# Moving part of a kernel's input loads to another DMA queue, with a different split over rows

## The chip, the cores and the metric

The kernel runs on one core of one Trainium2 chip. The metric is device time in microseconds (us), the median of several runs. A core has five engines that run their own instruction streams: TensorE (PE in the profile; its weight loads are PEld), VectorE (DVE), ScalarE (ACT), GpSimd (POOL) and SyncE (SP). Beside them sixteen DMA engines carry data between HBM and the on-chip memory. A DMA is issued by one of the instruction streams and then cut into packets, which the sixteen engines work off.

## The reference

For 1024 batch rows there are 32 fields of 128 numbers. For each of the 496 pairs of fields i < j the kernel multiplies field i by a 128x128 matrix that belongs to the pair, and multiplies the result elementwise by field j.

```python
# r_inputs: (1024, 32, 128) f32     L0_rec_W: (496, 128, 128) f32
v_i = inputs[:, I_IDX, :]
v_j = inputs[:, J_IDX, :]
transformed = jnp.einsum('bpd,ped->bpe', v_i, W)
return transformed * v_j            # (1024, 496, 128) f32
```

The output is 1024 x 496 x 128 x 4 bytes = 260.05 MB. The inputs are 16.8 MB (fields) and 32.5 MB (matrices). Almost all of the traffic is output.

## The kernel before

The host has transposed the data: a field is a tile of 128 partitions (rows) with 1024 numbers each, so one row of a field is 4 KB, and one field is 512 KB. Pairs are worked off in the order i = 30, 29, ... 0, so that field i is first needed when its row of pairs begins, and each field is loaded once, into a tile of its own.

```python
def _pairs():
    return [(i, j) for i in range(NF - 2, -1, -1) for j in range(i + 1, NF)]
...
xpool = ctx.enter_context(tc.tile_pool(name="x", bufs=1))
rpool = ctx.enter_context(tc.tile_pool(name="wr", bufs=5))
opool = ctx.enter_context(tc.tile_pool(name="o", bufs=4))
ppool = ctx.enter_context(tc.tile_pool(name="ps", bufs=8, space=bass.MemoryType.PSUM))
...
def load_x(f, n=1, pieces=1, eng=None):
    t = xpool.tile([P, n, BT], F32, tag=f"x{f}", name=f"x_{f}")
    s = BT // pieces
    for k in range(pieces):
        (eng or nc.sync).dma_start(out=t[:, :, k * s : (k + 1) * s], in_=xt[:, f : f + n, k * s : (k + 1) * s])
    ...
def load_w(c, splits=(0, WL)):        # WL = 4 matrices, 256 KB, 2 KB a row
    ...
        nc.sync.dma_start(out=w_raw[c][:, a:b, :], in_=wt[c, :, a:b, :])
```

The first eight fields (31 down to 24) and four groups of matrices are loaded ahead of the loop. The loop counts half pairs: u = 2q + h is half h (512 of 1024 columns) of pair q. A product in full precision takes three matmuls on split operands (the first 15 pairs use one native matmul). GpSimd does most of the splitting.

```python
def second(u):
    ...                                # third matmul into po[u]
    if k == 0 and h == 0:
        ots[g] = opool.tile([P, OG, BT], F32, tag="ot", name=f"ot_{g}")   # OG = 2 pairs, 1 MB, 8 KB a row
    nc.vector.tensor_tensor(ots[g][:, k, s], po.pop(u), x_sb[j][:, s], ALU.mult)
    ...
    elif k == OG - 1 and h == 1:
        nc.sync.dma_start(out=out[g], in_=ots[g])

for u in range(2 * NQ + LAG):          # NQ = 496
    q = u // 2
    if u % (2 * WL) == 0 and (q // WL + WLEAD) * WL < NQ:
        load_w(q // WL + WLEAD)
    if u < 2 * NQ:
        i, j = pairs[q]
        if u % 2 == 0 and j == i + 1 and 0 <= i - 2 - XLEAD:   # XLEAD = 5
            load_x(i - 2 - XLEAD)      # fields 23 down to 0
        first(u)
    if u >= LAG:
        second(u - LAG)
    ...                                # one split of matrices or of a field
```

So each group of two pairs takes four VectorE multiplications and ends in one 1 MB output DMA; four output tiles are in turn. The in-loop loads of fields 23 to 0 are issued at u = 0, 2, 6, 12, 20, 30, ... 506, 552 (of 992), seven rows of pairs ahead of their use.

Of the kernel before, what the change touches and what calls it, by code (L numbers as in the profile page):

```python
# [1 line left out]

# [4 lines left out]

F32 = mybir.dt.float32
F32R = mybir.dt.float32r
ALU = mybir.AluOpType  # L10

P = 128
NF = 32
NQ = NF * (NF - 1) // 2
BT = 1024
HB = 512
WC = 2
WL = 4
OG = 2
EPS = 2.0**-12  # L20
NATIVE = 5
SHARED = 10
XDLAG = 10
LAG = 3
WLEAD = 4
XLEAD = 5


def _pairs():

    return [(i, j) for i in range(NF - 2, -1, -1) for j in range(i + 1, NF)]


@with_exitstack
def kernel(
    ctx: ExitStack,
    tc: tile.TileContext,
    xt: bass.AP,
    wt: bass.AP,
    out: bass.AP,  # L40
):

    nc = tc.nc
    pairs = _pairs()
    nchunk = NQ // WC  # L60

    xpool = ctx.enter_context(tc.tile_pool(name="x", bufs=1))
    spool = ctx.enter_context(tc.tile_pool(name="xs", bufs=2))
    rpool = ctx.enter_context(tc.tile_pool(name="wr", bufs=5))
    wpool = ctx.enter_context(tc.tile_pool(name="ws", bufs=4))
    opool = ctx.enter_context(tc.tile_pool(name="o", bufs=4))
    ppool = ctx.enter_context(tc.tile_pool(name="ps", bufs=8, space=bass.MemoryType.PSUM))

    x_sb = {}
# [6 lines that stand above are left out]
            (eng or nc.sync).dma_start(out=t[:, :, k * s : (k + 1) * s], in_=xt[:, f : f + n, k * s : (k + 1) * s])  # L76
        for k in range(n):
            x_sb[f + k] = t[:, k, :]

    w_raw = {}  # L80

    def load_w(c, splits=(0, WL)):
        w_raw[c] = rpool.tile([P, WL, P], F32, tag="w", name=f"w_{c}")
        for a, b in zip(splits, splits[1:]):
            nc.sync.dma_start(out=w_raw[c][:, a:b, :], in_=wt[c, :, a:b, :])  # L85

    w_s = {}

    def split_w(c, u):

        k = c * WC % WL
        raw = w_raw[c * WC // WL][:, k : k + WC, :].rearrange("p q e -> p (q e)")
        h, l, d = [wpool.tile([P, WC * P], F32R, tag=t, name=f"{t}_{c}") for t in ("wh", "wl", "wd")]
        nc.scalar.mul(h, raw, 1.0 - 2.0**-13)  # L94
        nc.gpsimd.tensor_tensor(l, raw, h.bitcast(F32), ALU.subtract)  # L95
        nc.gpsimd.tensor_scalar(d, h.bitcast(F32), EPS, 1.0, ALU.mult, ALU.mult)  # L96
        nc.gpsimd.tensor_tensor(d, l.bitcast(F32), d.bitcast(F32), ALU.subtract)  # L97
        w_s[c] = (h, l, d)

    x_s = {}  # L100
    later = []

    def split_x(f, a, u):

        if a == 0:
            x_s[f] = [spool.tile([P, BT], F32R, tag=t, name=f"{t}_{f}") for t in ("xh", "xl", "xd")]
        s = slice(a, a + HB)
        h, l, d = [t[:, s] for t in x_s[f]]
        nc.scalar.mul(h, x_sb[f][:, s], 1.0 - 2.0**-13)  # L109
        nc.gpsimd.tensor_tensor(l, x_sb[f][:, s], h.bitcast(F32), ALU.subtract)  # L110
        nc.gpsimd.tensor_scalar(l, l.bitcast(F32), 1.0 / EPS, 1.0, ALU.mult, ALU.mult)  # L111
        if f > NF - 2 - NATIVE - SHARED:
            later.append((min(u + XDLAG, 2 * first_q[f] + LAG - 1), d, h.bitcast(F32), l.bitcast(F32)))
        else:
            nc.gpsimd.tensor_tensor(d, h.bitcast(F32), l.bitcast(F32), ALU.subtract)  # L115

    nq0 = NATIVE * (NATIVE + 1) // 2
    c0 = nq0 // WC
    first_q = {i: q for q, (i, j) in reversed(list(enumerate(pairs)))}

    todo = []
    for c in range(c0, nchunk):
        todo.append(((c - 3) * WC + 1, max(c * WC, nq0), lambda u, c=c: split_w(c, u)))
    for i in range(NF - 2 - NATIVE, -1, -1):
        for a in range(0, BT, HB):
            todo.append((first_q[i + 1] + 1 if i < NF - 3 - NATIVE else 2, first_q[i], lambda u, i=i, a=a: split_x(i, a, u)))
    todo.sort(key=lambda t: t[1])

    load_w(0, (0, 1, WL))
    load_x(NF - 2, pieces=2, eng=nc.scalar)
    load_x(NF - 1, pieces=2, eng=nc.scalar)
    load_x(NF - 3)
    load_x(NF - 4)
    load_w(1)
    for f in range(NF - 5, NF - 4 - XLEAD, -1):
        load_x(f)
    load_w(2)
    load_w(3)  # L140


    ctx.enter_context(tc.manual_schedule())
    po, ots = {}, {}


    def first(u):
        q, h = divmod(u, 2)
        i, c = pairs[q][0], q // WC
        r = slice(q % WC * P, (q % WC + 1) * P)  # L150
        s = slice(h * HB, (h + 1) * HB)
        po[u] = ppool.tile([P, HB], F32, tag="po", name=f"po_{u}")
        if q < nq0:
            nc.tensor.matmul(po[u], w_raw[q // WL][:, q % WL, :], x_sb[i][:, s], start=True, stop=True)  # L154
        else:
            for t in (0, 1):
                nc.tensor.matmul(po[u], w_s[c][t][:, r], x_s[i][t][:, s], start=t == 0, stop=t == 1)  # L157
            nc.scalar.mul(po[u], po[u], 1.0 + EPS)  # L158

    def second(u):  # L160
        q, h = divmod(u, 2)
        i, j = pairs[q]
        r = slice(q % WC * P, (q % WC + 1) * P)
        s = slice(h * HB, (h + 1) * HB)
        if q >= nq0:
            nc.tensor.matmul(  # L166
                po[u], w_s[q // WC][2][:, r], x_s[i][2][:, s], start=False, stop=True, skip_group_check=True
            )
        g, k = divmod(q, OG)
        if k == 0 and h == 0:  # L170
            ots[g] = opool.tile([P, OG, BT], F32, tag="ot", name=f"ot_{g}")
        nc.vector.tensor_tensor(ots[g][:, k, s], po.pop(u), x_sb[j][:, s], ALU.mult)  # L172
        if q >= NQ - 2:
            nc.sync.dma_start(out=out[g, :, k, s], in_=ots[g][:, k, s])
        elif k == OG - 1 and h == 1:
            nc.sync.dma_start(out=out[g], in_=ots[g])

    for u in range(2 * NQ + LAG):
# [3 lines that stand above are left out]
        if u < 2 * NQ:  # L182
            i, j = pairs[q]
            if u % 2 == 0 and j == i + 1 and 0 <= i - 2 - XLEAD:
                load_x(i - 2 - XLEAD)
            first(u)
        if u >= LAG:
            second(u - LAG)
        if u % 2 == 1:
            ready = [t for t in todo if t[0] <= q]  # L190
            if ready:
                ready[0][2](u)
                todo.remove(ready[0])
        while later and later[0][0] <= u:
            nc.vector.tensor_tensor(*later.pop(0)[1:], ALU.subtract)  # L195
    assert not todo and not later


# [25 lines left out]
```

## Time and profile before

The median of three runs is 768.14 us (766.21 to 768.76). The profiled execution has a span of 769.8 us.

| engine | busy us | share of the span |
|---|---|---|
| PE (matmul) | 722.7 | 94% |
| ACT | 638.7 | 83% |
| DVE | 632.0 | 82% |
| POOL | 593.2 | 77% |

The busy time of an engine is the union of its instructions' times. That of PE is modelled for pipelined matmuls and overstates how near PE is to its peak. The DMA engines are not in this table; the page reports them by slices and by queue. All in-loop loads and all stores are issued by SyncE, and so lie in one hardware queue (q1), which spreads every transfer over the sixteen DMA engines[...].

### The profile page before, as it was taken

The page shows a single profiled execution, that of the slowest core. Times are in us where ns is not written, and L with a number is a line of the kernel's source. Part 1 is how long each engine was busy: PE and PEld are TensorE (multiplying, and loading weights), DVE is VectorE, ACT ScalarE, POOL GpSimd, SP SyncE. Part 2 cuts the span into 40 slices and gives each one's busy share as a digit, 9 for nine tenths or more (in the row PEclk, how much of TensorE's full clock was granted, in tenths as well). Part 3 has the DMA queues.
Part 4 walks back from the last instruction along what each step waited for, and adds up shares of the span by engine and source line. Part 5 has one row for each costly group of instructions (what it writes and reads, how often), then busy time and mean ns, then how long its engine had stood idle before and what let it go on. Part 6 is the DMA issues. An engine that isn't in the chain of part 4 may idle for free.

```text
span 769.8 us, 11824 instructions
## 1 busy us (share of the span) xinstructions
PE 722.7 (94%) x2946; PEld 545.4 (71%) x2946; DVE 632.0 (82%) x1012; ACT 638.7 (83%) x1256; POOL 593.2 (77%) x863
## 2 busy tenths in 40 slices
PE   7988999999999999999999989999999999999994
PEld 3556766677777676777777767777777777777773
DVE  4869888888888788888888878888888888888885
ACT  2276988888888898888888889998988898998983
POOL 2677998887889878878878696978786969697660
PEclk9999999999999999999999999999999999999998
DMA  9999999999999999999999999999999999999997
GB/s 352 424 419 384 407 397 410 405 400 406 410 405 403 400 409 416 409 379 421 411 414 407 412 403 406 411 407 408 415 410 395 408 410 409 409 408 405 400 401 307
DMA packets 59108, 310.11 MB, mean 403 GB/s; under 512 B 6560, under 2 KB 6816, under 8 KB 27424
## 3 DMA queue, kind: packets, MB, share of 16 engines
q1 hardware_dynamic: 58464, 308.31, 99.4%
q10 hardware_dynamic: 576, 1.05, 0.4%
q8 instruction: 24, 0.39, 0.2%
q14 instruction: 44, 0.36, 0.1%
HBM read 49.28 MB, written 260.05 MB: 402 GB/s over the span
## 4 chain that ended last, share of the span: by engine, by line
DMA 61%; DVE 21%; PE 15%; issue 2%; DVEq 0%; SPq 0%; ACT 0%
DMA out_dram<-ot 60%; DVE ot L172 19%; PE po L157 9%; PE po L166 4%; DVE xd L195 2%; PE po L154 1%; DMA x<-in_xt_dram 1%; DVEq L172 0%; SPq L85 0%; DVEq L217 0%; ACT po L158 0%; DVEq L195 0%
## 5 line engine op out<-in xcount | busy, mean ns | idle before, releaser
L172 DVE TENSOR_TENSOR ot<-po,x 128x512 f32<-128x512 f32 x992 | 618.6, 684 | 129.5 <-DMA out_dram<-ot 70.2
L158 ACT ACTIVATE po<-po 128x512 f32<-128x512 f32 x962 | 551.2, 583 | 106.5 <-PE po L157 53.3
L157 PE MATMUL po<-xh,wh 128*128 128x512 f32 x962 | 388.7, 404 | 24.4 <-DVE ot L172 21.6
L166 PE MATMUL po<-xd,wd 128*128 128x512 f32 x962 | 376.9, 392 | 5.7 <-DVE xd L195 5.7
L157 PE MATMUL po<-xl,wl 128*128 128x512 f32 x962 | 377.6, 392 | 2.2 <-POOL wl L95 2.1
L157 PEld LDWEIGHTS po<-xh,wh 128*128 128x128 f32 x962 | 180.9, 188 | 110.2 <-DVE ot L172 72.5
L95 POOL TENSOR_TENSOR wl<-w,wh 128x256 fp32r<-128x256 f32 x241 | 179.2, 744 | 92.1 <-ACT wh L94 90.7
L166 PEld LDWEIGHTS po<-xd,wd 128*128 128x128 f32 x962 | 181.0, 188 | 46.3 <-ACT po L158 3.8
L157 PEld LDWEIGHTS po<-xl,wl 128*128 128x128 f32 x962 | 181.1, 188 | 36.8 <-POOL wl L95 4.5
L97 POOL TENSOR_TENSOR wd<-wl,wd 128x256 fp32r<-128x256 f32 x241 | 180.0, 747 | 20.1
L96 POOL TENSOR_SCALAR wd<-wh 128x256 fp32r<-128x256 f32 x241 | 99.1, 411 | 20.3
L94 ACT ACTIVATE wh<-w 128x256 fp32r<-128x256 f32 x241 | 99.2, 412 | 0.5 <-DMA w<-in_wt_dram 0.5
L110 POOL TENSOR_TENSOR xl<-x,xh 128x512 fp32r<-128x512 f32 x52 | 67.3, 1293 | 19.8 <-ACT xh L109 19.5
L115 POOL TENSOR_TENSOR xd<-xh,xl 128x512 fp32r<-128x512 f32 x32 | 41.4, 1292 | 2.7
L109 ACT ACTIVATE xh<-x 128x512 fp32r<-128x512 f32 x52 | 32.5, 628 | 10.5 <-DMA x<-in_xt_dram 10.3
L111 POOL TENSOR_SCALAR xl<-xl 128x512 fp32r<-128x512 f32 x52 | 32.8, 631 | 4.6
L154 PE MATMUL po<-x,w 128*128 128x512 f32 x60 | 29.0, 645 | 4.1 <-DMA x<-in_xt_dram 4.1
L154 PEld LDWEIGHTS po<-x,w 128*128 128x128 f32 x60 | 12.1, 206 | 20.2 <-issue 13.9
L195 DVE TENSOR_TENSOR xd<-xh,xl 128x512 fp32r<-128x512 f32 x20 | 16.6, 831 | 0.0
L109 ACT ACT_TABLE_LOAD x1 | 1.3, 1283 | 2.6 <-issue 2.6
L211 POOL MEMSET const-float32-0.0<- 128x1 f32 x1 | 0.1, 98 | 0.2 <-issue 0.2
L211 POOL MEMSET const-bfloat16-1.0<- 128x1 bf16 x1 | 0.1, 101 | 0.0
(2 smaller groups left out, 0.2 us busy)
## 6 DMA issues: line engine op xcount, KB each, us to landing
out_dram<-ot SPq DMA_DIRECT2D x247, 1024.0 KB, 8.9
w<-in_wt_dram SPq DMA_DIRECT2D x123, 256.0 KB, 9.1
x<-in_xt_dram SPq DMA_DIRECT2D x30, 512.0 KB, 9.5
x<-in_xt_dram ACTq DMA_DIRECT2D x4, 256.0 KB, 5.1
out_dram<-ot SPq DMA_DIRECT2D x4, 256.0 KB, 7.0
w<-in_wt_dram SPq DMA_DIRECT2D x1, 192.0 KB, 3.6
w<-in_wt_dram SPq DMA_DIRECT2D x1, 64.0 KB, 2.9
```

Of the source, the lines that this page charges most:

```text
L94: nc.scalar.mul(h, raw, 1.0 - 2.0**-13)
L95: nc.gpsimd.tensor_tensor(l, raw, h.bitcast(F32), ALU.subtract)
L96: nc.gpsimd.tensor_scalar(d, h.bitcast(F32), EPS, 1.0, ALU.mult, ALU.mult)
L97: nc.gpsimd.tensor_tensor(d, l.bitcast(F32), d.bitcast(F32), ALU.subtract)
L109: nc.scalar.mul(h, x_sb[f][:, s], 1.0 - 2.0**-13)
L110: nc.gpsimd.tensor_tensor(l, x_sb[f][:, s], h.bitcast(F32), ALU.subtract)
L115: nc.gpsimd.tensor_tensor(d, h.bitcast(F32), l.bitcast(F32), ALU.subtract)
L154: nc.tensor.matmul(po[u], w_raw[q // WL][:, q % WL, :], x_sb[i][:, s], start=True, stop=True)
L157: nc.tensor.matmul(po[u], w_s[c][t][:, r], x_s[i][t][:, s], start=t == 0, stop=t == 1)
L158: nc.scalar.mul(po[u], po[u], 1.0 + EPS)
L166: nc.tensor.matmul(po[u], w_s[q // WC][2][:, r], x_s[i][2][:, s], start=False, stop=True, skip_group_check=True)
L172: nc.vector.tensor_tensor(ots[g][:, k, s], po.pop(u), x_sb[j][:, s], ALU.mult)
```

## The change

The 24 fields that the loop loads are no longer loaded by one SyncE DMA of 128 rows. Rows 0 to 119 are loaded by a DMA that GpSimd issues ([...], in a queue of its own), and rows 120 to 127 by a small DMA of SyncE. The aim is to split these loads over the DMA engines in another way than the other transfers and to take them out of SyncE's queue. The bytes are the same, as are the tiles and the place in program order.

```diff
+XROWS = 120
...
+    def load_x_by_two(f):
+
+        t = xpool.tile([P, BT], F32, tag=f"x{f}", name=f"x_{f}")
+        nc.gpsimd.dma_start(out=t[:XROWS], in_=xt[:XROWS, f, :])
+        nc.sync.dma_start(out=t[XROWS:], in_=xt[XROWS:, f, :])
+        x_sb[f] = t
...
             if u % 2 == 0 and j == i + 1 and 0 <= i - 2 - XLEAD:
-                load_x(i - 2 - XLEAD)
+                load_x_by_two(i - 2 - XLEAD)
             first(u)
```

## The prediction

> **What bounds the kernel now.** I read the page's slices and queues first, then the chain, then the waits, and then stretches of the loop.
>
> ```profile
> DMA  9999999999999999999999999999999999999997
> GB/s 352 424 419 384 407 397 410 405 400 406 410 405 403 400 409 416 409 379 421 411 414 407 412 403 406 411 407 408 415 410 395 408 410 409 409 408 405 400 401 307
> q1 hardware_dynamic: 58464, 308.31, 99.4%
> ```
>
> The sixteen DMA engines have a packet in hand all the time, but they do not always move equally much: 424 and 419 GB/s in the second and third slice, some 408 later. Same busy share, 4% less moved, so packets got longer. That gap is what I want to explain. The chain of work by time shows how the DMA sets the pace:
>
> ```profile
> 516.95 2.50 DVE ot L172 x4
> 519.45 0.02 issue
> 519.47 8.95 DMA out_dram<-ot
> 528.41 0.03 issue
> 528.44 0.05 DVEq L172
> ...
> 744.18 0.23 PE po L166
> 744.41 0.71 PE po L157 x2
> ```
>
> Four multiplications fill an output tile (2.50 us), its store takes 8.95 us, and the chain goes on with the multiplication that needs the tile back. Four tiles are in turn, so one round of 16 multiplications takes about 11.5 us. The wait list says the same (first column: who waited for whom, total us, times, longest):
>
> ```profile
> DVE ot L172 <- DMA out_dram<-ot: 70.2, 83, 2.1
> DVE ot L172 <- PE po L166: 30.3, 34, 1.6
> ```
>
> Where no store holds it (744 us), the compute side needs 0.68 us a multiplication (0.23 for L166 and 0.45 for the mean pair of L157). The pace of the loop, from the multiplications in two stretches, one with field loads and one without:
>
> ```profile
> L172 DVE TENSOR_TENSOR ot<-po,x x263: 678/681/693, 199.5 to 399.4; 128x512 f32<-128x512 f32 x132
> L76 SPq DMA_DIRECT2D x<-in_xt_dram x7: 894/1097/1240, 203.9 to 371.0; - x7
> L172 DVE TENSOR_TENSOR ot<-po,x x277: 678/682/693, 499.9 to 699.4; 128x512 f32<-128x512 f32 x139
> ```
>
> The last times are those of the first and last start. From 500 us on: 199.5 / 276 = 0.723 us a multiplication. From 200 to 400 us: 199.9 / 262 = 0.763.
>
> Now the packets. In the trace an undisturbed 8 KB packet (a row of a store) starts 306 ns after the one before it on its engine, a 4 KB one (a row of a field) 156, a 2 KB one (a row of matrices) 81. Each transfer gives every engine 8 rows. One multiplication stands for a quarter of a store and an eighth of a matrix load: 2 x 306 + 81 + 2 (completion packets) = 0.695 us. A field load is 8 x 156 + 6 = 1.254 us. So the pace should be 0.695, and it is 0.723; with loads (199.9 - 7 x 1.254) / 262 = 0.729. I use 0.725: 0.030 us, 4%, is lost on each multiplication.
>
> **Where the 4% goes.** Each transfer ends with sixteen semaphore increments, one from each DMA engine, all in the trace. Sorted within each transfer, the median of the first is 4.66 us ahead of the last, the thirteenth is 3.65 ahead and the fifteenth still 2.03. One engine trails all others, by about 0.6 us at 20 to 40 us and about 4.5 at 60 to 80 us, and then by about as much to the end. In the late increments its increment comes some 500 ns after the completion packet, against some 350 on the others, so it looks like the same engine each time. Packets followed up to such last increments are often 314 to 340 ns long instead of 309 (mean about 322 where I could follow them); its 4 KB and 2 KB packets are not. So one engine is 4% slow on stores, and with four output tiles in turn the other fifteen run ahead about 4.6 us and then wait for it. On the leading engines the first 4 KB packet of a field load is often stretched to 500 to 1300 ns, which fits a queue that had just run dry. The DMA share of 99% hides this[...].
>
> [...]
>
> **The change part by part.** It removes 24 field loads from q1: on each engine 24 x 1.254 = 30.1 us. It adds the same on fifteen engines by GpSimd's queue, and one row (156 + 6 ns) 24 times = 3.9 us on eight of them. [...]
>
> 1. Loop up to the last field load (u = 552). Before, the slow engine sets it: 552 x 0.725 + 30.1 = 430.3 us. After, the other fifteen set it: 552 x 0.695 + 30.1 + 3.9 = 417.6. The slow one needs only 552 x 0.725 = 400.2, so it runs ahead until the output tiles stop it, about 4.6 us by the lead seen before: it is done at 413.0. Gain on it: 17.3 us.
> 2. The remaining 440 multiplications: the slow engine takes 440 x 0.725 = 319.0, as before, and the others 305.8. The others start later by 4.6 us and are still done 8.6 earlier, so the slow one ends last again and nothing more is won or lost.
> 3. GpSimd issues 24 more DMAs. [...] it waits for ACT 90.7 us now. Off the path. SyncE has 24 issues as before, of 32 KB now.
> 4. Start: GpSimd has nothing to wait for and issues fields 23 and 22 in the first microseconds, beside the first fields. 2 x 0.48 MB at 420 GB/s is 2.3 us on the first loads. As the queues are full until stores begin at 14.3 us, this reorders work more than it adds. I take 1 us at most.
>
> Sum: 768.1 - 17.3 + 1 = about 752 us. The compute side (0.68 a multiplication) stays below 0.695 and does not take over, though with 0.015 us to spare.
>
> **The rivals.**
> - The engine left out moves round, or the slow one is not the one left out. If it moves round, each engine is left out 24/16 = 1.5 times and saves 1.9 us; if the slow one is among the lowest eight, it carries 3.9 us more: 766 to 773 us. [...]
> - The 4% are not one engine's but HBM's, and the trailing engine is a symptom. For it: mean packet times per lane are near one another. Then nothing is won, 766 to 771. Against it: 424 GB/s in the early slices, while the trailing engine had not yet fallen back.
> - A second engine takes the bound. Two engines trail by 1.2 to 2.2 us for long from 100 to 480 us. If they are held by their own speed, the first part gains only that gap, and most of the gain falls to the second part: 755 to 760. Against it: their packets that I could follow are 309 ns flat.
> - GpSimd becomes late: [...] It is 83 to 86% busy from 60 to 300 us. [...]
> - The load was hidden anyway, as nobody waits for in-loop fields. True for latency, but the DMA engines are full, so it's their time that counts.
>
> **Range and chances.** I give 65% to the slow engine being spared: then 746 to 759, around 751. Else 765 to 774. The median of both is near 755. Faster by 2% means below 752.8, a bit over half of the first case and none of the second: 0.40. Slower by 2% (over 783.5) needs GpSimd to get in the way badly: 0.05.
>
> **What would show it.** Right: the DMA slices rise from 408 to 415 or more from the fourth slice on; 0.70 to 0.71 us a multiplication up to about 420 us apart from the loads; the trailing engine's lag gone or turned round while fields are loaded, and back at 4 to 5 us late in the run; DVE waits less for the stores than 70.2 us in the first half. A software queue appears with 24 x 0.49 MB = 11.8 MB. Wrong: the same 408 GB/s and the same lag (not the spared engine), or waits of PE for GpSimd's splits well above the 6.6 us of now (4.5 and 2.1), or DVE waiting for fields in the loop.
>
> I predict 755 us, 743 to 771.

## The result

The changed kernel takes 776.54 us (median of four runs, 775.03 to 777.75), the kernel before 767.55 on the same chip: a ratio of 1.0117, 95% interval 1.0086 to 1.0147. That is 9.0 us lost where the prediction expected about 13 us won (768.1 to 755). Differences below are what a run's ratio is above 1, times 767.5 us, since the baseline moves a little from session to session.

### The profile page after: what moved, and what is told of

It is laid out like the page before. It is cut to its first block, busy times and chain, and to the rows that moved or that the text cites. A ratio compares the mean times of both kernels' runs of the same rounds, so it can differ in the third digit from the quotient of the medians.

```text
span 776.0 us, 11892 instructions
## 1 busy us (share of the span) xinstructions
PE 722.3 (93%) x2946; PEld 543.9 (70%) x2946; DVE 633.0 (82%) x1012; ACT 638.7 (82%) x1256; POOL 607.1 (78%) x887
## 3 DMA queue, kind: packets, MB, share of 16 engines
q0 software_dynamic: 3456, 11.80, 4.9%
## 4 chain that ended last, share of the span: by engine, by line
DMA 50%; PE 26%; DVE 17%; POOL 3%; issue 2%; DVEq 0%; ACT 0%; SPq 0%; POOLq 0%; ACTq 0%
DMA out_dram<-ot 48%; DVE ot L180 16%; PE po L165 16%; PE po L174 7%; PE po L162 3%; DMA x<-in_xt_dram 1%; POOL wl L103 1%; DVE xd L203 1%; POOL xd L123 1%; POOL xl L118 0%; POOL wd L105 0%; POOL xl L119 0%; DVEq L180 0%; POOL wd L104 0%; ACT wh L102 0%
## 5 line engine op out<-in xcount | busy, mean ns | idle before, releaser
L203 DVE TENSOR_TENSOR xd<-xh,xl 128x512 fp32r<-128x512 f32 x20 | 18.2, 908 | 0.0
L84 POOL DMA_DIRECT2D x<-in_xt_dram x24 | 14.3, 596 | 0.9 <-POOLq L219 0.8
```

## The profile after

From the page of the changed kernel, the slices, the queues and the shares of the chain:

```profile
GB/s 300 402 408 419 409 408 405 408 396 401 407 418 391 400 400 418 402 379 415 408 407 398 411 391 400 407 412 406 409 403 401 400 413 408 409 408 407 401 397 303
...
q1 hardware_dynamic: 55392, 296.51, 94.4%
q0 software_dynamic: 3456, 11.80, 4.9%
...
DMA 50%; PE 26%; DVE 17%; POOL 3%; issue 2%; DVEq 0%; ACT 0%; SPq 0%; POOLq 0%; ACTq 0%
```

The 11.80 MB went to the software queue as foreseen. Nothing else of the hoped-for picture is there. The first two slices fell from 352 and 424 to 300 and 402 GB/s, and the later ones stayed near 408. The waits hardly moved, so no new wait took over:

```profile
DVE ot L180 <- DMA out_dram<-ot: 73.9, 85, 2.2
...
PEld po L165 <- POOL wl L103: 6.7, 9, 1.0
...
PE po L165 <- POOL wl L103: 3.4, 7, 0.7
```

VectorE still waits for the stores, and TensorE waits 10.1 us for GpSimd's splits, against 6.6. GpSimd's 24 issues took 596 ns each, 14.3 us in all.

The same two stretches as before, with and without field loads:

```profile
L180 DVE TENSOR_TENSOR ot<-po,x x261: 680/681/693, 199.5 to 399.9; 128x512 f32<-128x512 f32 x131
L84 POOL DMA_DIRECT2D x<-in_xt_dram x7: 592/592/594, 205.4 to 375.3; - x7
...
L180 DVE TENSOR_TENSOR ot<-po,x x276: 680/681/693, 499.6 to 699.5; 128x512 f32<-128x512 f32 x138
```

Without loads the pace is 199.9 / 275 = 0.727 us a multiplication (0.723 before). With loads, less 7 x 1.254 us, it is (200.4 - 8.8) / 260 = 0.737 (0.729 before). The 0.008 us x 260 are 2.1 us, 0.3 us for each load; as the stretch without loads is 0.004 us slower too, 0.15 to 0.3 us belong to a load. So a part of the loss is paid load by load. The start holds the other part. The timeline (start, duration, engine, line; in brackets what it waited for), first the kernel before, then the changed one:

```profile
8.07 0.69 DVE L172 TENSOR_TENSOR ot<-po,x 128x512 f32<-128x512 f32 x1 [8.07 <-DMA x<-in_xt_dram]
```

```profile
1.26 1.27 POOL L84 DMA_DIRECT2D x<-in_xt_dram  x2 [0.81 <-POOLq L219]
...
4.29 6.35 SPq L77 DMA_DIRECT2D x<-in_xt_dram  x4
...
11.65 0.69 DVE L180 TENSOR_TENSOR ot<-po,x 128x512 f32<-128x512 f32 x1 [11.65 <-DMA x<-in_xt_dram]
```

GpSimd issues fields 23 and 22 at 1.26 us, and the first multiplication runs at 11.65 us instead of 8.07. From 5 to 12.5 us the 4 KB packets of both queues took 230 to 240 ns on average, where an undisturbed one takes 159.

**Which engine trails.** This is the decisive reading. A DMA of eight rows is followed by nine recorded updates. The first, here at about 1.4 us, comes 3 us or more ahead of the next, and I take it for the issuing side's; the other eight I take for one increment each of eight DMA engines. Times from issue, in us, for three of the changed kernel's eight-row DMAs:

```
issued at 282.5   1.33 | 4.41  4.51  4.58  4.60  4.71  4.81  4.85  10.20
issued at 344.1   1.40 | 5.85  5.90  6.33  6.42  6.48  6.75  7.15  10.48
issued at 408.7   1.39 | 4.80  4.95  5.02  5.06  5.15  5.61  5.72  10.06
```

Seven engines are close together and the eighth increment comes 3 to 5 us later. In all 14 such DMAs from 100 us on this gap is 1.8 to 5.4 us, in the ten before at most 1.8. The eighth increment also comes 0.2 to 0.7 us after the last one of SyncE's DMA before it, so I take the same engine to be the last there. The trailing engine is one of the eight that the small DMA of SyncE uses. It was not left out; it got one row more. In the 120-row DMAs of GpSimd one of the sixteen increments comes about 2 us ahead of the rest (0.4 to 3.2, median 2.3), and in the stores issued from 36 to 62 us one engine leads the last by 4.6 to 6.1 us, with all others within 1.5 to 2.5. One load left out saves an engine 1.25 us, so a lead of 4.6 to 6.1 us is, as I read it, that of one fixed engine. So the DMA of GpSimd does leave out the same engine each time, only it is not the one that trails.

A second sign tells a slow engine from one that is merely late: the step from the last increment of a store or matrix load to that of the store after it. From 100 to 450 us its median is 2.58 us in the kernel before and 2.60 in the changed one, while eight undisturbed 8 KB packets take 8 x 306 ns = 2.45 us. I take the engine that trails in both for a slow one, with about 323 ns a packet (2.58 us / 8).

## Experiments

My theory after the result: each load puts one more row on the trailing engine (24 x 0.162 = 3.9 us), and the first two GpSimd loads cost the start. Rivals: the software queue itself costs the time, or SyncE's extra issues do.

**The split without the software queue.**

```diff
-        nc.gpsimd.dma_start(out=t[:XROWS], in_=xt[:XROWS, f, :])
+        nc.sync.dma_start(out=t[:XROWS], in_=xt[:XROWS, f, :])
```

> Both parts (rows 0 to 119 and 120 to 127) of the 24 in-loop fields are issued by SyncE, so the split stays and the software queue goes. Theory (the slow DMA engine is one of those that carry the eight rows, and each load puts one more row on it): 24 x 0.162 = 3.9 us more than before, 770 to 773 us, and the last increment of the eight-row DMA trails the others of it by 2 us or more from about 80 us on. Rival 1 (the software queue costs it all): 766 to 769, as before. Rival 2 (the slow engine would be the one left out, and only the software queue spoils it): 750 to 758.

778.63 us, 1.0139 (1.0117 to 1.0162), 10.7 us more than before. The rival that blames the software queue alone is out, and so is the hope that the engine left out is the trailing one. But it is far more than the 3.9 us of the extra row. The stretch from 20 to 60 us, here and then in the kernel before (columns: length, busy time and count by engine, clock, DMA share, GB/s):

```profile
20.00:60.00 40.00, 34.42 (x116) 20.74 (x114) 26.62 (x44) 20.47 (x40) 26.61 (x38) 1.00 1.01 390
```

```profile
20.00:60.00 40.00, 35.14 (x120) 21.77 (x118) 30.43 (x48) 20.22 (x41) 28.81 (x41) 1.00 1.02 422
```

The same DMA share moved 390 instead of 422 GB/s. In the trace, 81% of the 4 KB packets from 20 to 30 us took over 200 ns (mean 259), against none before (mean 159). A 120-row transfer of SyncE gives fifteen increments and a 128-row one sixteen, so its rows go to the engines in another way. That its packets get in each other's way is my reading; where they would meet was shown by no run.

**The software queue without the split.**

```diff
-                load_x(i - 2 - XLEAD)
+                load_x(i - 2 - XLEAD, eng=nc.gpsimd)
```

> All 128 rows of the in-loop fields are issued by GpSimd in one DMA: the software queue stays and the split goes. Theory: no extra row, so only what the early start of fields 23 and 22 and the queue itself cost: 769 to 773 us. Rival 1 (software queue costs it all): as the changed kernel, 775 to 778, with the first multiplication about 3 us later. Rival 2 (split costs it all): 766 to 769.

768.46 us, 1.0016 (1.0000 to 1.0032): 1.2 us. With 128 rows GpSimd's queue costs next to nothing, and the early loads do little harm. Its timeline:

```profile
1.27 1.28 POOL L76 DMA_DIRECT2D x<-in_xt_dram  x2 [0.81 <-POOLq L211]
...
9.03 0.69 DVE L172 TENSOR_TENSOR ot<-po,x 128x512 f32<-128x512 f32 x1 [9.03 <-DMA x<-in_xt_dram]
```

Issued at the same 1.27 us, the same two fields put the first multiplication at 9.03 us and not at 11.65, and the 4 KB packets of 5 to 12.5 us take 161 and 163 ns on average in the two queues. So it is not the early issue alone that costs the start, but the 120-row split beside 128-row loads.

**Early and late loads apart.** First only fields 16 to 0 changed, then only 23 to 17, then all but the first two:

```diff
-                load_x_by_two(i - 2 - XLEAD)
+                (load_x_by_two if i - 2 - XLEAD <= 16 else load_x)(i - 2 - XLEAD)   # sw_late
+                (load_x_by_two if i - 2 - XLEAD > 16 else load_x)(i - 2 - XLEAD)    # sw_early
+                (load_x_by_two if i - 2 - XLEAD <= 21 else load_x)(i - 2 - XLEAD)   # start2
```

> Fields 23 to 17 (issued up to u = 42) are loaded by SyncE as before, only fields 16 to 0 as in the changed kernel. If the late start of the first multiplication (11.6 for 8.1 us) is what counts, the time is near before: 767 to 770 us. If it is a cost of each load in the steady loop (0.3 us by the progress of the multiplications from the 64th to the 600th), 17 x 0.3 = 5 us stay: 772 to 774, with the first multiplication again at 8.1 us.

> The complement of the kernel with the late fields: fields 23 to 17 as in the changed kernel, 16 to 0 by SyncE as before. If the cost is made of a late start (3.6 us, from packets of both queues that take 230 instead of 160 ns in the first 12 us) and of one extra row a load, this has the start and 7 x 0.162 = 1.1 us: 771 to 773. If the start is made good later, as the progress of the multiplications up to the 64th suggests, 768 to 770.

> The changed kernel, but fields 23 and 22, which GpSimd issues in the first two us, are loaded by SyncE as before; the other 22 stay as changed. If the late start comes from these two loads meeting SyncE's first loads in the same DMA engines, the first multiplication is back at 8.1 us and about 3.6 us are won of the changed kernel's 9: 771 to 774. If the start does not matter in the end: 775 to 778.

Late: 771.85 us, 1.0048 (1.0029 to 1.0066), 3.7 us or 0.22 a load. Early: 772.20, 1.0069 (1.0054 to 1.0084), 5.3 us. They add up to the whole 9.0. Without the first two: 774.22, 1.0074 (1.0047 to 1.0100), 5.7 us or 0.26 a load. Its timeline shows the start mended:

```profile
3.83 12.61 PE L162 MATMUL po<-x,w 128*128 128x512 f32 x24 [3.83 <-DMA x<-in_xt_dram]
...
7.69 0.69 DVE L180 TENSOR_TENSOR ot<-po,x 128x512 f32<-128x512 f32 x1 [7.69 <-PE po L162]
```

The start is therefore worth some 3 to 4 us of the 9.0 (9.0 - 5.7, and 5.3 less seven loads of 0.22), and the rest is a cost of each load.

**Which engine: unequal tails.** All by SyncE, rows 120 to 127 as 7+1, 6+2, 5+3 or 4+4 by the field's number:

```diff
+        if m == 0:
+            nc.sync.dma_start(out=t[XROWS:127], in_=xt[XROWS:127, f, :])
+            nc.sync.dma_start(out=t[127:], in_=xt[127:, f, :])
+        ...                                # m == 1, 2, 3: 6+2, 5+3, 4+4 rows
```

> All by SyncE: rows 0 to 119, then the last eight rows as 7+1, 6+2, 5+3 or 4+4 rows by the field's number modulo 4. A DMA of n rows should give n increments by DMA engines. If the engines are the lowest-numbered n, the trailing increment (2 us or more after the one before it) is in all DMAs of at least m rows and in none of fewer, and the slow engine is the m-th. If it is the eighth, it is in none of these and only in the 120-row DMAs; the time is then near before (766 to 769), or lower if the eighth gets less than the rest. If the engines used are not a fixed set, the trailing increment comes and goes.

778.04 us in a single run. The number of increments was as expected, n for n rows and fifteen for 120 rows. From 233 us on the engine that comes last is in every tail of two or more rows and in none of one, so it is the second of the set, if each smaller set is the beginning of a larger one. I took it for the slow one, which was wrong: from 300 to 450 us the step between last increments is 2.48 us, and not 2.58 as in the kernel before. If the sets begin with the same engines, the two tails gave the first ones two rows of a field; my reading is that one of them had fallen behind through that load.

**Extra rows, first attempt.** Beside each of fields 16 to 0 three copies of n rows from HBM to a spare tensor in HBM; the kernel's own work is as before:

```diff
+        for r in range(3 if f <= 16 else 0):
+            nc.sync.dma_start(out=spare[k : k + ROWS, :], in_=xt[P - ROWS :, f, :])   # ROWS = 8, 2, 1
```

> The kernel before, with three extra DMAs of SyncE beside each of fields 16 to 0: each copies 8 rows of 4 KB from HBM to a spare place in HBM that nobody reads. If a DMA of 8 rows puts one row on each of the first eight DMA engines and the slow engine is one of them, its 51 rows cost 51 x 0.162 = 8.3 us: 775 to 777. If the slow engine is not among them, or all engines have room, the time stays within 2 us of before.

> The same with 2 rows a copy. The trace with unequal tails points to the slow engine as the second of the row: then 51 rows more on it cost 8.3 us, as with 8 rows, 775 to 777. If it is the third to eighth, the first two engines have room for 8.3 us and the time is that of before within 2 us.

> The same with 1 row a copy, so only the first engine gets more. If the slow engine is the second: within 2 us of before, 766 to 769. If it is the first: 775 to 777. If the one row is cut into pieces for all sixteen engines, about half a us more.

788.58 us (1.0275, 1.0258 to 1.0292), 786.15 (1.0251, 1.0235 to 1.0267) and 781.72 (1.0188, 1.0173 to 1.0203). All missed. The single row was cut into sixteen pieces of 256 bytes, 0.2 MB for all 51 copies, and yet it cost 14.4 us. SyncE's own timeline in that run shows why:

```profile
253.61 1.40 SPq L97 DMA_DIRECT2D w<-in_wt_dram  x1
255.06 1.40 SPq L78 DMA_DIRECT2D x<-in_xt_dram  x1
256.51 4.41 SPq L89 DMA_DIRECT2D spare_dram<-in_xt_dram  x3
261.02 1.00 SPq L188 DMA_DIRECT2D out_dram<-ot  x2
```

Five loads in a row hold SyncE from 253.6 to 261.0 us, and the next store waits behind them. The fourth run of the next set gives the same tiny copies to GpSimd:

```diff
-            nc.sync.dma_start(out=spare[k : k + ROWS, :], in_=xt[P - ROWS :, f, :])
+            nc.gpsimd.dma_start(out=spare[k : k + ROWS, :], in_=xt[P - ROWS :, f, :])
```

> The 51 copies of one row (cut into sixteen pieces of 256 bytes, next to no DMA time) issued by GpSimd instead of SyncE. If their 14.8 us came from SyncE's stream, where stores wait behind an issue that takes about 1.4 us, the time falls back to within 3 us of before. If each small DMA costs the DMA engines 0.29 us by itself, it stays at 780 to 783.

770.71 us, 1.0033 (1.0011 to 1.0056): 2.5 us are left of 14.4. Most of the cost was SyncE's stream and not the DMA engines.

**Extra rows, one issue.** One copy per field, with n runs of 3067 numbers (12,268 bytes; 3067 is a prime number, which I hoped would keep a single run whole):

```diff
+        if f <= 16:
+            nc.sync.dma_start(
+                out=spare[k : k + ROWS, :],          # ROWS = 1, 2, 8; then 7, 4
+                in_=xt[P - ROWS :, 24:27, :].rearrange("p f b -> p (f b)")[:, :3067],
+            )
```

> The kernel before, with one extra DMA of SyncE beside each of fields 16 to 0: it copies one run of 12,268 bytes from HBM to a spare place in HBM. A single run of a prime number of elements should go to one DMA engine alone (one increment). The runs with tiny copies cost 0.29 us for each extra SyncE issue, so 17 x 0.29 = 4.9 us is the floor: 771 to 773 if the first engine is not the slow one. If it is, 17 x 3 x 0.156 = 8.0 us come on top: 779 to 781.

> The same copy with two runs of 12,268 bytes, for the first two engines. If the slow engine is one of them: 779 to 781. If it is the third to eighth: 771 to 773, as with one run.

> The same copy with eight runs of 12,268 bytes, for the first eight engines. The eight-row DMAs of the changed kernel all had the trailing increment, so the slow engine is among them: 779 to 781. If what one engine carries more does not matter, and only the issue does: 771 to 773.

> The same copy as before with seven runs of 12,268 bytes, for the first seven engines. One and two runs cost nothing and eight cost 6.8 us. If the slow engine is the eighth, seven cost nothing: 766 to 769. If it is one of the third to seventh: 773 to 776.

> The same copy with four runs of 12,268 bytes, for the first four engines. Two runs cost nothing, seven cost about 7 us. If the slow engine is the third or fourth: 773 to 776. If it is the fifth to seventh: 766 to 769.

| runs of 12 KB a copy | us | ratio (interval) | more than before, us |
|---|---|---|---|
| 1 | 766.47 | 0.9992 (0.9973 to 1.0012) | -0.6 |
| 2 | 767.14 | 1.0000 (0.9984 to 1.0015) | 0.0 |
| 4 | 767.08 | 0.9999 (0.9969 to 1.0028) | -0.1 |
| 7 | 774.60 | 1.0082 (1.0046 to 1.0119) | 6.3 |
| 8 | 774.30 | 1.0088 (1.0063 to 1.0113) | 6.8 |

The increments were 1, 2, 4, 7 and 8, so I take n runs to go to n engines. Four engines take seventeen more packets of 460 ns each (the median in the trace) at no cost; seven do not. The eighth adds nothing that the intervals show: it is a step, as one engine makes it, and not a slope with the bytes, on which four runs would cost 3.4 us (their interval ends at 2.1).

The traces show which engine comes last. Where a copy's last increment follows that of the load beside it by about one packet (median 0.5 us), the last engine is one of the copy's. With seven runs this is so for all 17 copies and with eight for 13, from 118 us on, at a step of 2.58 us from 100 to 450 us: so I place the slow engine in these sets. With one, two and four runs it is so too, for 13, 12 and 17 of the 17 copies, but at a step of 2.46 to 2.48 us: there an engine that is not slow has come to be the last under the copies, at no cost in the median. So the last engine is not the same in every execution, and it is the pace and not the last place that names the slow one.

With the issue the same in all five, and the step from 0 to 6.3 us between four and seven, the slow engine is the fifth, sixth or seventh of the set. This takes a smaller set to be the beginning of a larger one, and the slow engine to be the same on two chips (one, two and eight runs were measured on one, four and seven on another). Its time is the kernel's: 17 x 0.46 = 7.8 us put on it cost 6.3 to 6.8, or 0.13 us for 4 KB. The floor of 4.9 us that I expected for the issue was not there: one more SyncE issue a load is free, three in a row are not.

**Tails of seven and one rows.** Built on the guess of the eighth engine, which the seven-run copy of the same set refuted:

```diff
-        nc.sync.dma_start(out=t[XROWS:], in_=xt[XROWS:, f, :])
+        nc.sync.dma_start(out=t[XROWS : P - 1], in_=xt[XROWS : P - 1, f, :])
+        nc.sync.dma_start(out=t[P - 1 :], in_=xt[P - 1 :, f, :])
```

> The changed kernel with its last eight rows as seven rows and one row, both by SyncE: [...] If the slow engine is the eighth and its extra row is what each load costs, 24 x 0.13 to 0.16 = 3 to 4 us go away: 772 to 774, with the late start left. If the extra row does not matter, as the changed kernel: 775 to 778.

> The same tails, but fields 23 to 17 by SyncE as before, so neither the late start nor an extra row on the eighth engine is left. If these two are the whole cost: 766 to 769, as before. If the split by the software queue costs by itself: 769 to 772.

779.95 us, 1.0152 (1.0111 to 1.0192), and with fields 23 to 17 by SyncE 771.31, 1.0050 (1.0028 to 1.0073). Seven rows still reach the slow engine (in both traces the tail of seven holds the last increment from 104 us on, at a step of 2.60 us), so its row stays, and the second figure is that of the late fields with one tail (771.85). The first is 2.7 us above the changed kernel, but the intervals overlap.

**An attempt at the gain.** Fields 16 to 7 in 119, 7 and 2 rows, to take load off the engines from the eighth on:

```diff
+        for a, b in ((0, 119), (119, 126), (126, P)):
+            nc.sync.dma_start(out=t[a:b], in_=xt[a:b, f, :])
```

> The kernel before, but fields 16 to 7 by SyncE as 119, 7 and 2 rows, [...] If the eighth is the slow one that bounds the kernel, its work falls by 10 x 1.25 = 12.5 us and the first seven, with about 30 us of room, get 17 us more: 754 to 760. If three SyncE issues in a row or rows that collide on the memory side eat it up: 764 to 775.

787.29 us, 1.0241 (1.0193 to 1.0290), 18.5 us more. It was built on the same guess. How many engines shared the 119 rows, and whether the slow one did, was not shown. The stretch from 60 to 120 us in it:

```profile
60.00:120.00 60.00, 52.57 (x207) 40.04 (x206) 48.55 (x75) 46.07 (x93) 47.63 (x66) 0.93 0.93 363
```

The DMA share falls to 0.93 (0.99 in the kernel before) and the rate to 363 GB/s (396). I read it so that some engines ran dry while others, with more rows, still worked.

## Why the prediction was wrong

- **What bounds the kernel** held in the main. One DMA engine is slow by its pace (a step of 2.58 us for 2.45), and what is put on it is paid nearly in full (0.13 of the 0.156 us a row), while four others take the same for nothing (-0.1 us). But it is not always the last: with all rows in GpSimd's queue, and with only the late fields changed, the step from 100 to 450 us is 2.47 us too. And the 4.5 us at 60 to 80 us, read as its distance from all others, is that from the first; the last but one was only 1.9 us ahead. The 0.68 us of the compute side stand: the line of 0.71 us for two matmuls is an outlier among 0.45 to 0.46.
- **The step that failed** is the condition on which step 1 stood: that the slow engine is spared. That one engine is left out each time fits the trace (an increment about 2 us ahead in GpSimd's DMAs, a lead of 4.6 to 6.1 us in the stores). That it is the slow one is wrong. By the table of copies the slow engine is the fifth, sixth or seventh of the set that small DMAs of SyncE use, so it kept its eight rows and got one more. The 17.3 us of step 1 therefore fall away whole. I had weighed this rival (35%) and priced it at 3.9 us for the extra row; by the 0.13 us of the copies it is 3.1.
- **Which engines.** The trace does not number the engines. "The lowest eight" in the rivals, and "the first n engines" in the expectations, are my names for those that a small DMA of SyncE uses; that these are the same ones each time, and that a smaller set is the beginning of a larger one, is my assumption. What was counted are the increments: 16 for 128 rows and for GpSimd's 120, 15 for 120 rows by SyncE, and 8, 7, 4, 2 and 1 for as many rows or long runs.
- **The start** was put at 1 us at most and is 3 to 4. The step that failed is "this reorders work more than it adds": where loads of both splits met, 4 KB packets took 230 to 240 ns for 159. With 128 rows in the same place the whole change costs 1.2 us.
- **Each load** costs 0.22 to 0.26 us, of which the extra row would explain 0.13 to 0.16; no run took away that row alone. The rest, 1.5 to 3 us in all, stays open. It is not the software queue as such (1.2 us with 128 rows); the split's disturbed packets may be it, as in the run with SyncE alone. A tail of 4+4 rows alone, which by the table of copies should keep the row off the slow engine, was not tried.
- **The rivals.** GpSimd being late did not come about (10.1 us of waits for 6.6; an issue took 596 ns of it). The engine left out did not move round, by the lead of 4.6 to 6.1 us in the stores. A second engine taking the bound was not put to the test, as the first was never relieved; that engines of normal pace came last in several traces (steps of 2.46 to 2.48 us) speaks for it, so even the right engine spared might win less than 17.3 us. The rival that the trailing engine is only a symptom does not fit the step in the table of copies, nor the slow engine's own pace.
- Why that engine is slow is open, and so is a version that beats both: no split that I tried is shown to have given the slow engine fewer rows than before, and I had no transfer that spares it and loads the rest. GpSimd with all 128 rows is no better than before (768.46 us).

## What to carry to other kernels

When all DMA engines are busy (99% of the time here) and the loop is held by buffers, look at the sixteen increments of each transfer: one engine may set the pace, and then only its packets count (here 17 long packets on it cost 6.3 us, and on four others nothing). The last place alone did not name it; the step from one last increment to the next did (2.58 us, against 2.46 to 2.48). Before sparing an engine, find out which one it is, with a copy to an increasing number of engines that nobody waits for; sparing the wrong one won nothing here, and the leftover rows that land on the right one cost (0.13 us a 4 KB row, by the copies). A load of 128 rows is worth keeping whole, since with another split the same bytes took longer packets here (259 ns for 159).

## What had not been expected of the hardware

- Queueing several loads on SyncE is not free: each of the five in the view above held its stream for about 1.4 us, and three extra in a row cost 14.4 / 51 = 0.28 us each of kernel time, with almost no bytes, while one extra cost nothing.
- 4 KB packets of a 120-row load by SyncE took 259 ns on average at 20 to 30 us, those of a 128-row load 159.
- A single row of 4 KB from HBM to HBM was cut into sixteen pieces of 256 bytes, while a single run of 3067 numbers (12,268 bytes) gave one increment, and a packet of this size took 460 ns.
- An engine of normal pace was the last of the sixteen for 13 of 17 copies with one run a copy, and the kernel was not slower for it (766.47 us).
